# Layer 3's output stage in source order on three engines, with transposes one step behind normalizing and the first image read back during the convolution

## The chip, the cores and the metric

The kernel runs on one core of a Trainium2 chip. The metric is the device time of one execution in microseconds; the time of a kernel is the median of its runs. Names of engines as in the profile: PE is TensorE (PEld its weight loads), DVE is VectorE, ACT is ScalarE, POOL is GpSimd, SP is SyncE, which here only issues transfers.

## The reference

Eight images of 56 x 56 pixels with 192 channels go through four layers, each of the form x + layer(group norm(x)). Only the last matters here:

```python
def _L3_conv_ref(x, dw_kernel, dw_bias, ln_gamma, ln_beta, w0, b0, w1, b1, gamma):
    y = lax.conv_general_dilated(x, dw_kernel, (1, 1), 'SAME', feature_group_count=192, ...) + dw_bias
    mu = jnp.mean(y, axis=-1, keepdims=True)
    var = jnp.mean(jnp.square(y - mu), axis=-1, keepdims=True)
    y = (y - mu) * lax.rsqrt(var + EPS) * ln_gamma + ln_beta
    y = jnp.einsum('bhwc,cd->bhwd', y, w0) + b0
    y = jax.nn.gelu(y, approximate=False)
    y = jnp.einsum('bhwd,dc->bhwc', y, w1) + b1
    return y * gamma
...
x = x + _L3_conv_ref(_gn(x), ...)
```

The convolution is depthwise, 7 x 7. The layer norm goes over the 192 channels of each pixel. w0 widens 192 channels to 768, w1 narrows them again. All is float32.

## The kernel before, in words

One program does all four layers in stages, each with its own pools of tiles in SBUF and PSUM. A scheduler places the instructions of each engine: it takes them by priority as their inputs and their buffers come free by its own model of time, so the order on an engine is not that of the source. Each engine then works its queue in order. The pools hand out buffers by name: `bufs=2` means that the third tile of a name waits for the last use of the first.

Two stages of layer 3 are concerned.

**The convolution** (`convolve`, L988 to L1023). A loop over 12 groups of 16 channels. For each group SP loads the band matrix `wt` (4 MB, L997) and eight pieces `zc`, one for each image (L1002), from DRAM. PE does 64 matmuls (L1009), 16 for each four channels, for all images at once; DVE and ACT copy the sums to `yc` (L1019, L1021); SP writes `yc` to DRAM as `yd[b]`, one transfer of 224 KB for each image (L1023). `yd[b]` has 128 rows: the two halves of an image's row pairs with 64 places each. 28 columns (`NPAIR`) for each channel are pairs of image rows.

**The output stage** (L1297 to L1317). w0, w1 and the bias `dwb` are loaded on POOL's queue. `layer3_load` reads all 192 channels of one image back (`yl`, 2688 KB, two buffers), `layer3_image` reads its residual `x`. `layer3_norm` is a generator that yields between steps, so that the caller can strew it between others' work. For one image it

- adds the bias on POOL in four pieces (L1043),
- takes statistics of each of 28 columns on DVE (`bn_stats`, L189), one yield for each four,
- turns them into mean and variance with six small DVE instructions for all columns (`ln_var`, L196 to L203),
- takes the square root on ACT (L209), and reciprocal and shift on DVE (`ln_rows`, L210, L212),
- and for four blocks of four columns (two halves each; the last block has two): scales on DVE (`yt`, L1058, eight instructions), transposes on PE in three groups of four (`tp`, L1065, two PSUM buffers) and copies with scale and shift on ACT to `y` (L1076).

`layer3_out` takes an image in four tiles of 392 columns. In a tile, for six values of m, PE does 12 matmuls (`ph`, L1087) and ACT the Gelu (`hid`, L1091); after each second m the caller's `between` runs one step of the next image's `layer3_norm`. Then PE does three sums of 12 matmuls (`po`, L1098), ACT scales (`z`, L1103), DVE adds the residual (L1105), and SP writes the result (L1108). `ph` has two PSUM buffers, so the matmuls of m + 2 wait for the Gelu of m. In the trace each of these matmuls is two records, so a tile is 72 records of `ph` and 72 of `po`.

Square root and Gelu are in different function tables of ACT, so that a table load stands at each change between them. In the order that the scheduler made, the steps of images run ahead of the source: while image b is put out, the norm of image b + 1 is finished and that of image b + 2 begun, up to its square root, in ACT's queue ahead of the Gelus of image b.

Of the kernel before, what the change touches and what calls it, by code (L numbers as in the profile page):

```python
# [27 lines left out]
DPERM = [128 * c + 32 * (s % 4) + i for cs, ss in PASSES[:2] for s in ss for c in cs for i in range(32)]  # L28
DPERM += range(512, D1)
HEADS, HD, WN = 6, 32, 49  # L30
C2 = 384
EXP = 768

# [43 lines left out]
def kernel(ctx: ExitStack, tc: tile.TileContext, a: dict, out: bass.AP):  # L77
# [24 lines left out]
    def vec(name, i=0, rows=128):  # L102
        o = VOFF[name] + i
        return vecs[0:rows, o:o + 1]
# [78 lines left out]
    def run(steps):  # L183
        for _ in steps:
            pass

    def ln_pieces(st, yl, ns):
        for n in ns:
            nc.vector.bn_stats(st[:, n], yl[:, :, n])  # L189

    def ln_var(st, P, nch, pool):

        mean = pool.tile([P, NPAIR], F32, name="ln_mean")
        nc.vector.tensor_tensor(mean, st[:, :, 1], st[:, :, 4], ALU.add)  # L196
        d = pool.tile([P, NPAIR], F32, name="ln_d")
        nc.vector.tensor_tensor(d, st[:, :, 1], st[:, :, 4], ALU.subtract)
        nc.vector.tensor_tensor(d, d, d, ALU.mult)
        var = pool.tile([P, NPAIR], F32, name="ln_var")  # L200
        nc.vector.tensor_tensor(var, st[:, :, 2], st[:, :, 5], ALU.add)
        nc.vector.tensor_scalar(var, var, 1.0 / nch, None, ALU.mult)
        nc.vector.scalar_tensor_tensor(var, d, 0.25, var, ALU.mult, ALU.add)  # L203
        return mean, var

    def ln_rows(mean, var, P, eps, pool):

        rs = pool.tile([P, NPAIR], F32, name="ln_rs")
        nc.scalar.activation(rs, var, AF.Sqrt, bias=eps[0:P])  # L209
        nc.vector.reciprocal(rs, rs)  # L210
        mr = pool.tile([P, NPAIR], F32, name="ln_mr")
        nc.vector.scalar_tensor_tensor(mr, mean, -0.5, rs, ALU.mult, ALU.mult)  # L212
        return rs, mr


    def toeplitz_rows(psum, pool, rows):
# [676 lines left out]
    def layer2_norm(k, ml, rs, mr, pool, psum):  # L893


        n0 = 4 * k
        nn = min(4, PH - n0)
        nt = 2 * W * nn
        y = pool.tile([128, 3, 2, 8 * W], F32, name="y2")
        for s in range(2):  # L900
            yt = pool.tile([2 * W, 4, C2], F32, name="yt2")
            for i in range(nn):
                n = PH * s + n0 + i
                if i % 2 == 0:
                    nc.vector.tensor_scalar(yt[:, i], ml[:, :, n], rs[:, n:n + 1], mr[:, n:n + 1], ALU.mult, ALU.add)
                else:
                    nc.scalar.activation(yt[:, i], ml[:, :, n], AF.Identity, bias=mr[:, n:n + 1], scale=rs[:, n:n + 1])  # L907
            for m in range(3):
                tp = psum.tile([128, 4, 2 * W], F32, name="tp2")
                for i in range(nn):  # L910
                    nc.tensor.transpose(tp[:, i], yt[:, i, 128 * m:128 * m + 128], ident[0:2 * W, 0:2 * W])  # L911
                nc.scalar.activation(
                    y[:, m, s, 0:nt], tp[:, 0:nn].rearrange("p i n -> p (i n)"), AF.Identity,
                    bias=vec("be2", m), scale=vec("g2", m),
                )
        return y
# [68 lines left out]
                    to(zt[0:64, :, 1 + PH], tp[0:64, n2, 0], 1)  # L985
            nc.sync.dma_start(zd[b][:, 64 * j:64 * j + 64], zt)

    def convolve():  # L988

        band = a["band"]  # L990
        with ExitStack() as st:
            pool = st.enter_context(tc.tile_pool(reuse_waits="tile", name="cv", bufs=2))
            psum = st.enter_context(tc.tile_pool(reuse_waits="tile", name="cvp", bufs=3, space=PSUM))
            for g in range(C // CG):
# [26 lines left out]
                            nc.scalar.copy(dst, src)  # L1021
                for b in range(nimg):
                    nc.sync.dma_start(yd[b][:, cs], yc[:, b])  # L1023

    def layer3_load(b, pool):
        yl = pool.tile([OP, C, NPAIR], F32, name="yl")
        nc.sync.dma_start(yl, yd[b])
        return yl

    def layer3_image(b, pool):  # L1030
        x = pool.tile([128, 3, NH], F32, name="x3")
# [3 lines left out]
    def layer3_norm(yl, pool, psum, dwb):  # L1035


        y = pool.tile([128, 3, NH], F32, name="y3")
        yield y
        st = pool.tile([OP, NPAIR, 6], F32, name="ln_st")  # L1040
        for n in range(0, NPAIR, 7):
            ys = yl[:, :, n:n + 7]
            nc.gpsimd.tensor_tensor(ys, ys, dwb.unsqueeze(2).to_broadcast([OP, C, 7]), ALU.add)  # L1043
        for n in range(0, NPAIR, 4):
            yield
            ln_pieces(st, yl, range(n, n + 4))
        rows = ln_var(st, OP, C, pool)
        yield
        rs, mr = ln_rows(*rows, OP, eps6, pool)
        for i0 in range(0, PH, 4):  # L1050
            yield
            ni = min(4, PH - i0)

            yt = pool.tile([OP, 4, 3, 2, 64], F32, name="yt3")
            for i in range(ni):
                for s in range(2):
                    n = PH * s + i0 + i
                    nc.vector.tensor_scalar(  # L1058
                        yt[:, i, :, s], yl[:, :, n].rearrange("p (j c) -> p j c", j=3),
                        rs[:, n:n + 1], mr[:, n:n + 1], ALU.mult, ALU.add,  # L1060
                    )
            for j in range(3):
                tp = psum.tile([128, 4, OP], F32, name="tp3")
                for i in range(ni):
                    nc.tensor.transpose(  # L1065
                        tp[:, i], yt[:, i, j].rearrange("p s c -> p (s c)"), ident[0:OP, 0:OP]
                    )

                src = tp[:, 0:ni].rearrange("p i (s w) -> p i s w", s=2)
                dims = [list(z) for z in src.ap]  # L1070
                src = bass.AP(
                    src.tensor, src.offset + OP - 1,
                    [dims[0], dims[1], [-dims[2][0], 2], [-dims[3][0], W]],
                )
                dst = y[:, j, 2 * W * i0:2 * W * (i0 + ni)].rearrange("p (i s w) -> p i s w", s=2, w=W)
                nc.scalar.activation(dst, src, AF.Identity, bias=vec("be3", j), scale=vec("g3", j))  # L1076

    def layer3_out(b, y, x, pool, psum, between):

# [171 lines left out]
    with ExitStack() as st:  # L1251
# [5 lines left out]
        ml = [layer2_load(b, pool) for b in range(min(2, nimg))]  # L1257
        x = [load_halves(pool, x2[0], "x2o")]
        ln_pieces(ml[0][1], ml[0][0], range(NPAIR))
        rows = ln_rows(*ln_var(ml[0][1], 2 * W, C2, pool), 2 * W, eps5, pool)  # L1260
        y = layer2_norm(0, ml[0][0], *rows, pool, psum)
        steps = iter(())
        for b in range(nimg):
            slot = [0]

            def between():

                i, slot[0] = slot[0], slot[0] + 1
                if b + 1 < nimg and i < 8:
                    ln_pieces(ml[b + 1][1], ml[b + 1][0], range(NPAIR * i // 8, NPAIR * (i + 1) // 8))  # L1270
                if b + 1 < nimg and i == 7:
                    following.append(ln_var(ml[b + 1][1], 2 * W, C2, pool))
                for _ in range(1 if i < 5 else 2):
                    next(steps, None)

            following = []
            for k in range(4):

                if k < 3:
                    ahead = layer2_norm(k + 1, ml[b][0], *rows, pool, psum)  # L1280
                elif b + 1 < nimg:
                    rows = ln_rows(*following[0], 2 * W, eps5, pool)
                    ahead = layer2_norm(0, ml[b + 1][0], *rows, pool, psum)
                if k == 2 and b + 1 < nimg:
                    x.append(load_halves(pool, x2[b + 1], "x2o"))
                if k == 3 and b + 2 < nimg:
                    ml.append(layer2_load(b + 2, pool))
                layer2_out(k, y, x[b], psum, w_out, between)
                y = ahead
            run(steps)  # L1290
            nc.sync.dma_start(xd[b], x[b])
            steps = layer3_in(b, x[b], zp, pool, psum)
        run(steps)


    convolve()
    with tc.tile_pool(reuse_waits="tile", name="l3o", bufs=2) as pool, tc.tile_pool(reuse_waits="tile", name="l3op", bufs=2, space=PSUM) as psum:  # L1297
        w0 = resident("w0", nc.gpsimd, pool)
        w1 = resident("w1", nc.gpsimd, pool)
        dwb = pool.tile([OP, C], F32, name="dwb", bufs=1)  # L1300
        nc.gpsimd.dma_start(dwb, a["dw_b"].partition_broadcast(OP))
        yl = [layer3_load(b, pool) for b in range(min(2, nimg))]
        x = [layer3_image(0, pool)]
        steps = layer3_norm(yl[0], pool, psum, dwb)
        y = [next(steps)]
        for _ in steps:
            pass
        for b in range(nimg):
            if b + 2 < nimg:
                yl.append(layer3_load(b + 2, pool))  # L1310
            if b + 1 < nimg:
                steps = layer3_norm(yl[b + 1], pool, psum, dwb)
                y.append(next(steps))
                x.append(layer3_image(b + 1, pool))
            layer3_out(b, y[b], x[b], pool, psum, lambda: next(steps, None))
            for _ in steps:
                pass  # L1317

# [98 lines left out]
```

## Time and profile before

| | us |
|---|---|
| median of 3 runs | 6330.82 (6327.23 to 6345.44) |
| the profiled execution, its own time | 6351.08 |
| its span | 6349.2 |
| the convolution's matmuls (first to last) | 5072.0 to 5372.0 |
| first matmul `ph` of the output stage | 5418.1 |
| last matmul of the output stage | 6342.5 |
| PE busy over the span | 5569.1 (88%) |

Two stretches of the output stage, as busy time of PE in a stretch: from 5585 to 5609 us PE is busy 24.00 of 24 us at full clock, with nothing of the norm beside it; from 5664 to 5692 it is busy 19.31 of 28. In the convolution, from 5180 to 5330, PE is busy all but 0.3 us, at a DMA share of 0.90.

How to read it: a row of the timeline has start and length in us, engine, line, operation, output and inputs, their shapes, the number of instructions merged into it, and in brackets the idle time of that engine before it and what ended that time. A row of the waits has who waited, for whom, the sum in us, the number of times and the longest. A page's row of instructions has busy us and mean ns, then the idle time ahead of them with its releaser. Matmul ends are modelled, starts are measured.

### The profile page before, as it was taken

The numbers are of one execution on the slowest core, as the hardware profiler recorded it, in microseconds if no ns is written. First come the engines' busy times: TensorE is split into PE (matmuls) and PEld (weight loads), VectorE is DVE, ScalarE is ACT, GpSimd is POOL, SyncE is SP. The second block draws the span as 40 slices with busy tenths as digits, with TensorE's granted clock in tenths as the row PEclk, the third lists the DMA queues.
The fourth block names the chain that finished last, engine by engine and source line by source line (L and its number), as shares of the span: only waits on it lengthen the run. The fifth ranks groups of instructions, "written<-read, shape, count | busy, mean of one in ns | idle before, by whom it ended". The sixth has DMA issues, their size and how long they took to land. (4 is left out here: it accounts for less than half of the span.)

```text
span 6349.2 us, 126376 instructions
## 1 busy us (share of the span) xinstructions
PE 5569.1 (88%) x55636; PEld 3587.9 (57%) x55636; DVE 3439.3 (54%) x4752; ACT 2239.7 (35%) x2922; POOL 1302.1 (21%) x813
## 2 busy tenths in 40 slices
PE   6799989999999688888888598999588798789999
PEld 5677766666666345545445375777244498344444
DVE  5677765555665344444444486888688511532321
ACT  2334444443344233333332102555355300333333
POOL 1100034544444122122121102333110100110100
PEclk8899999999999888888888799999798799899999
DMA  6799886666665613444433675666667488121211
GB/s 166 185 221 210 188 262 263 260 253 240 240 252 194 88 33 55 60 58 63 55 48 44 103 266 208 224 228 233 153 203 208 170 305 305 64 67 56 70 54 27
DMA packets 1039131, 1013.10 MB, mean 160 GB/s; under 512 B 832104, under 2 KB 964372, under 8 KB 1011572
## 3 DMA queue, kind: packets, MB, share of 16 engines
q1 hardware_dynamic: 1028064, 954.17, 53.7%
q0 software_dynamic: 5648, 31.32, 1.5%
q10 hardware_dynamic: 4868, 19.52, 0.9%
q8 instruction: 437, 7.16, 0.5%
q14 instruction: 114, 0.93, 0.0%
HBM read 676.28 MB, written 345.08 MB: 161 GB/s over the span
## 5 line engine op out<-in xcount | busy, mean ns | idle before, releaser
L366 PE MATMUL qv<-w_qv_sb,xn 64*112 64x288 f32 x5376 | 722.2, 425 | 50.9 <-DVE act L372 47.6
L404 POOL COPY lc<-lt 128x896 f32<-128x896 f32 (+1 forms) x320 | 573.0, 1808 | 616.7 <-PE op L412 598.7
L366 PEld LDWEIGHTS qv<-w_qv_sb,xn 64*112 64x112 f32 x5376 | 535.5, 184 | 232.8 <-DVE act L372 64.7
L1087 PE MATMUL ph<-y,w_sb 64*128 64x392 f32 x2304 | 429.9, 511 | 49.1 <-ACT hid L1091 49.1
L373 ACT ACTIVATE act<-act 112x576 f32<-112x576 f32 x448 | 299.5, 682 | 461.7 <-DVE act L372 428.2
L1098 PE MATMUL po<-hid,w_sb 128*64 128x392 f32 x2304 | 395.1, 496 | 10.8 <-ACT hid L1091 10.8
L412 PEld LDWEIGHTS op<-rc,lc 128*56 128x56 f32 x9216 | 308.4, 136 | 127.6 <-issue 65.7
L412 PE MATMUL op<-rc,lc 128*56 128x56 f32 x9216 | 339.7, 222 | 46.0 <-POOL lc L404 24.2
L424 PE MATMUL pj<-xn,w_p_sb 64*128 64x392 f32 (+1 forms) x1920 | 373.0, 515 | 7.7 <-issue 4.7
L445 PE MATMUL y<-pp,w_o_sb 128*64 128x392 f32 (+1 forms) x1920 | 355.9, 503 | 20.4 <-DVE x L453 11.6
L372 DVE TENSOR_TENSOR act<-qv,b_qv 112x576 f32<-112x576 f32 x448 | 320.8, 751 | 86.1 <-PE qv L366 85.7
L1105 DVE TENSOR_TENSOR x<-x,z 128x392 f32<-128x392 f32 x96 | 55.8, 581 | 557.9 <-ACT z L1103 557.9
L1087 PEld LDWEIGHTS ph<-y,w_sb 64*128 64x128 f32 x2304 | 230.5, 194 | 224.1 <-ACT hid L1091 55.2
L404 ACT COPY rc<-rt 128x896 f32<-128x896 f32 (+1 forms) x160 | 256.9, 1606 | 230.7 <-PE op L412 216.0
L834 PE MATMUL cv<-zc,wt 128*128 128x224 f32 x1536 | 312.8, 355 | 27.9 <-DMA zc<-pd 27.9
L834 PEld LDWEIGHTS cv<-zc,wt 128*128 128x128 f32 x1536 | 290.5, 189 | 71.0 <-issue 54.9
L705 POOL TENSOR_TENSOR e<-e,mx 128x1176 f32<-128x1176 f32 x64 | 139.9, 2186 | 925.1 <-DVE mx L704 874.4
L655 PE MATMUL qk_ps<-xr,wg 64*96 64x392 f32 x1536 | 309.6, 511 | 14.9 <-ACT qk L661 13.3
L438 DVE TENSOR_TENSOR pp<-pp,ot 128x784 f32<-128x784 f32 (+1 forms) x160 | 154.6, 967 | 308.4 <-ACT pp L429 287.2
L1009 PE MATMUL cps<-zc,wt 128*128 128x224 f32 x1536 | 299.3, 356 | 23.1 <-DMA zc<-zd 22.5
L1009 PEld LDWEIGHTS cps<-zc,wt 128*128 128x128 f32 x1536 | 290.0, 189 | 32.5 <-issue 24.9
L847 POOL TENSOR_TENSOR rows<-rows,loc 128x896 f32<-128x896 f32 x96 | 228.1, 2377 | 390.2 <-ACT rows L843 262.8
(206 smaller groups left out, 9321.5 us busy)
## 6 DMA issues: line engine op xcount, KB each, us to landing
lt<-left SPq DMA_DIRECT2D x72, 1792.0 KB
rt<-right SPq DMA_DIRECT2D x72, 1792.0 KB
left<-qv SPq DMA_DIRECT2D x224, 252.0 KB
right<-qv SPq DMA_DIRECT2D x448, 126.0 KB
wt<-in_band_dram SPq DMA_DIRECT2D x24, 2048.0 KB
wt<-in_band_dram SPq DMA_DIRECT2D x12, 4096.0 KB
pd<-pt SPq DMA_DIRECT2D x8, 5568.0 KB
zc<-pd SPq DMA_DIRECT2D x192, 232.0 KB
```

Source lines behind the costliest of these rows:

```text
L366: nc.tensor.matmul(ps[s][:, which, 0:D1 // 2], xn[64 * s:64 * s + 64, j, bass.ts(i, 2 * W)], w_qv[64 * s:64 * s + 64, j, which, ns], start ...
L372: nc.vector.tensor_tensor(act, ps[s][:, :, 0:D1 // 2], b_qv[:, :, ns], ALU.add)
L373: nc.scalar.activation(act, act, AF.Silu)
L404: copy(c[:, 0:nu], raw.rearrange("p (w u d) -> p u d w", u=nu, d=64 // nu)[:, :, d0:d0 + 8])
L412: nc.tensor.matmul(op[64 * u:64 * u + W, i, :], lc[:, u, i], rc[:, u, i], start=True, stop=True)
L424: nc.tensor.matmul(ps[0:M, s, 0:TT], w_p[64 * s:64 * s + 64, j, d0:d0 + M], xn[64 * s:64 * s + 64, j, ts], start=(j == 0), stop=(j == 2),)
L445: nc.tensor.matmul(y[64 * s:64 * s + 64], w_o[0:M, c, 64 * j:64 * j + 64], pp[0:M, s], start=(c == gated[0][0]), stop=(c == gated[-1][0]),)
L655: nc.tensor.matmul(ps[s], wg[64 * s:64 * s + 64, j, c0:c0 + HC], xw[64 * s:64 * s + 64, j, gs], start=(j == 0), stop=(j == 2),)
L834: nc.tensor.matmul(dst, wt[:, c4 + i, 128 * q:128 * q + 128], zc[:, :, c4 + i, q:q + NPAIR], start=(q == 0), stop=(q == 1),)
L1009: nc.tensor.matmul(dst.rearrange("p (b n) -> p b n", n=NPAIR), wt[:, c4 + i, q * OP:(q + 1) * OP], zc[:, :, c4 + i, q:q + NPAIR], start=(q ...
L1087: nc.tensor.matmul(ps[:, s, 0:TT], w0[64 * s:64 * s + 64, j, m * 128:(m + 1) * 128], y[64 * s:64 * s + 64, j, ts], start=(j == 0), stop=(j ...
L1098: nc.tensor.matmul(ps[64 * s:64 * s + 64], w1[:, m, 64 * j:64 * j + 64], hid[:, m, s], start=(m == 0), stop=(m == 5),)
```

## The change

Four things are changed, all in layer 3.

1. `convolve` gets a tile `first` (image 0's `yl`) and `dwb`, both in a new pool on the other side of SBUF that lives from before the convolution. After each group's writes, POOL reads that group of image 0 back from DRAM and adds the bias to it. The whole load of image 0 on SP goes away. w0 and w1 stay on POOL's queue, and now stand behind the twelve read-backs and additions.
2. For image 0 (`dwb is None`) the norm works block by block: statistics, variance, root and scaling of four column pairs at a time. Its block 0 is done ahead of `layer3_out`, the others in `between` of tile 0.
3. In all images a block's transposes and copies come one step after its scaling; statistics go in five steps rather than seven. A norm of a later image has twelve steps, as many as `layer3_out` has calls of `between`.
4. `tc.manual_schedule` keeps PE, ACT and DVE in source order from there to the end; POOL and SP are still the scheduler's.

In the built order, for images 1 to 7, the root stands behind the Gelu of m = 1 in tile 2 of the image before, the transposes of block 0 behind m = 5 of tile 2, those of blocks 1, 2 and 3 behind m = 1, 3 and 5 of tile 3. On ACT a block's three copies stand directly behind the Gelus of those m. For image 0, the root of block k + 1 stands ahead of the copies of block k. The order of all stages before is the same as it was.

`ln_var` and `ln_rows` take their statistics with a halves axis (a view for layer 2), so that they can work on a part of the columns.

```diff
+IN_ORDER = {mybir.EngineType.PE, mybir.EngineType.Activation, mybir.EngineType.DVE}
...
-    def convolve():
+    def convolve(first, dwb):
...
                 for b in range(nimg):
                     nc.sync.dma_start(yd[b][:, cs], yc[:, b])
+                nc.gpsimd.dma_start(first[:, cs], yd[0][:, cs])
+                add_bias(first[:, cs], dwb[:, cs])
...
+    def add_bias(y, dwb):
+        nc.gpsimd.tensor_tensor(y, y, dwb.unsqueeze(2).to_broadcast(list(y.shape)), ALU.add)
...
     def layer3_norm(yl, pool, psum, dwb):
         y = pool.tile([128, 3, NH], F32, name="y3")
         yield y
         st = pool.tile([OP, NPAIR, 6], F32, name="ln_st")
-        for n in range(0, NPAIR, 7):
-            ys = yl[:, :, n:n + 7]
-            nc.gpsimd.tensor_tensor(ys, ys, dwb.unsqueeze(2).to_broadcast([OP, C, 7]), ALU.add)
-        for n in range(0, NPAIR, 4):
+        first = dwb is None
+        if not first:
+            for n in range(0, NPAIR, 7):
+                add_bias(yl[:, :, n:n + 7], dwb)
+            for k in range(5):
+                yield
+                ln_pieces(st, yl, range(NPAIR * k // 5, NPAIR * (k + 1) // 5))
+            rows = ln_var(in_halves(st), C, pool)
             yield
-            ln_pieces(st, yl, range(n, n + 4))
-        rows = ln_var(st, OP, C, pool)
-        yield
-        rs, mr = ln_rows(*rows, OP, eps6, pool)
-        for i0 in range(0, PH, 4):
+            rs, mr = ln_rows(*rows, eps6, pool)
+
+        def scaled(i0):
+            yt = pool.tile([OP, 4, 3, 2, 64], F32, name="yt3")
+            for i in range(min(4, PH - i0)):
+                for s in range(2):
+                    k = i if first else i0 + i
+                    nc.vector.tensor_scalar(
+                        yt[:, i, :, s], yl[:, :, PH * s + i0 + i].rearrange("p (j c) -> p j c", j=3),
+                        rs[:, s, k:k + 1], mr[:, s, k:k + 1], ALU.mult, ALU.add,
+                    )
+            return yt
+
+        ready = None
+        for i0 in range(0, PH + 4, 4):
             yield
...
+            if i0 < PH:
+                if first:
+                    ns = slice(i0, min(i0 + 4, PH))
+                    ln_pieces(st, yl, [PH * s + n for s in range(2) for n in range(ns.start, ns.stop)])
+                    rs, mr = ln_rows(*ln_var(in_halves(st)[:, :, ns], C, pool), eps6, pool)
+                following = scaled(i0)
+            if ready is not None:
+                i1 = i0 - 4
+                ni = min(4, PH - i1)
+                for j in range(3):
+                    tp = psum.tile([128, 4, OP], F32, name="tp3")
+                    for i in range(ni):
+                        nc.tensor.transpose(
+                            tp[:, i], ready[:, i, j].rearrange("p s c -> p (s c)"), ident[0:OP, 0:OP]
+                        )
...
+                    nc.scalar.activation(dst, src, AF.Identity, bias=vec("be3", j), scale=vec("g3", j))
+            ready = following
...
-    convolve()
-    with tc.tile_pool(reuse_waits="tile", name="l3o", bufs=2) as pool, tc.tile_pool(reuse_waits="tile", name="l3op", bufs=2, space=PSUM) as psum:
+    with ExitStack() as st:
+        lpool = st.enter_context(tc.tile_pool(reuse_waits="tile", name="l3y", bufs=2, side="right"))
+        dwb = lpool.tile([OP, C], F32, name="dwb", bufs=1)
+        nc.gpsimd.dma_start(dwb, a["dw_b"].partition_broadcast(OP))
+        yl = [lpool.tile([OP, C, NPAIR], F32, name="yl")]
+        convolve(yl[0], dwb)
+        pool = st.enter_context(tc.tile_pool(reuse_waits="tile", name="l3o", bufs=2))
+        psum = st.enter_context(tc.tile_pool(reuse_waits="tile", name="l3op", bufs=2, space=PSUM))
         w0 = resident("w0", nc.gpsimd, pool)
         w1 = resident("w1", nc.gpsimd, pool)
-        dwb = pool.tile([OP, C], F32, name="dwb", bufs=1)
-        nc.gpsimd.dma_start(dwb, a["dw_b"].partition_broadcast(OP))
-        yl = [layer3_load(b, pool) for b in range(min(2, nimg))]
         x = [layer3_image(0, pool)]
-        steps = layer3_norm(yl[0], pool, psum, dwb)
-        y = [next(steps)]
-        for _ in steps:
-            pass
+        if nimg > 1:
+            yl.append(layer3_load(1, lpool))
+        st.enter_context(tc.manual_schedule(engines=IN_ORDER))
+        own, steps = layer3_norm(yl[0], pool, psum, None), iter(())
+        y = [next(own)]
+
+        next(own), next(own), next(own)
+
+        def between():
+            next(own, None)
+            next(steps, None)
...
-            layer3_out(b, y[b], x[b], pool, psum, lambda: next(steps, None))
-            for _ in steps:
-                pass
+            layer3_out(b, y[b], x[b], pool, psum, between)
+            run(steps)
```

## The prediction, as put on record ahead of the result

> **What bounds the kernel now.** I read the page first, then the waits of each engine in layer 3's output stage (5372 to 6343 us), then the chain of waits there, then the timeline round the longest waits. The page says who is busy: the two matmul groups of this stage.
>
> ```profile
> span 6349.2 us, 126376 instructions
> ...
> L1087 PE MATMUL ph<-y,w_sb 64*128 64x392 f32 x2304 | 429.9, 511 | 49.1 <-ACT hid L1091 49.1
> ...
> L1098 PE MATMUL po<-hid,w_sb 128*64 128x392 f32 x2304 | 395.1, 496 | 10.8 <-ACT hid L1091 10.8
> ```
>
> The last column is TensorE's idle time: 59.9 us stand before ph and po, and Gelu (L1091) ends it. The waits of the stage show why Gelu is late, and a third idle time, for the first image's normalized rows:
>
> ```profile
> PE ph L1087 <- ACT hid L1091: 49.1, 6, 10.0
> PE tp L1065 <- DVE yt L1058: 40.8, 5, 39.4
> PE po L1098 <- ACT hid L1091: 10.8, 1, 10.8
> ACT ln_rs L209 <- DVE ln_var L203: 92.2, 8, 35.5
> ```
>
> ScalarE waits 92.2 us in the square root of layer norm. It is a queue in order, so Gelu stands behind. One such place, at the start of image 1:
>
> ```profile
> 5546.13 0.33 SPq L1027 DMA_DIRECT2D yl<-yd  x1
> 5555.79 10.70 POOL L1043 TENSOR_TENSOR yl<-yl,dwb 128x1344 f32<-128x1344 f32 x4 [109.51 <-DMA yl<-yd]
> 5572.33 0.32 ACT L209 ACTIVATE ln_rs<-ln_var,eps 128x28 f32<-128x28 f32 x1 [7.11 <-DVE ln_var L203]
> 5574.38 1.72 ACT L1091 ACTIVATE hid<-ph,vecs_sb 128x784 f32<-128x784 f32 x2
> 5575.35 4.91 PE L1087 MATMUL ph<-y,w_sb 64*128 64x392 f32 x18 [7.70 <-ACT hid L1091]
> ```
>
> The scheduler put the root of image b+2 (b = 1 here: image 3) ahead of the Gelus of image b. That image is loaded only once yl has a free buffer (5546), gets its bias on GpSimd, its statistics, and only then its root: TensorE stands 7.7 us, and more around it. The same row recurs at 5691, 5805, 5921 and 6037. Last, the start of the stage:
>
> ```profile
> 5372.63 0.53 ACT L1021 COPY yc<-cps 128x448 f32<-128x448 f32 x1 [5.62 <-DVE yc L1019]
> 5373.19 3.99 SPq L1023 DMA_DIRECT2D yd<-yc  x8
> 5377.29 1.16 SPq L1027 DMA_DIRECT2D yl<-yd  x2
> 5387.51 20.56 POOL L1043 TENSOR_TENSOR yl<-yl,dwb 128x1344 f32<-128x1344 f32 x8 [37.97 <-DMA yl<-yd]
> 5390.07 11.62 DVE L189 BATCH_NORM_STATS2 ln_st<-yl 128x6 f32<-128x192 f32 x28 [17.48 <-POOL yl L1043]
> 5418.09 1.67 PE L1087 MATMUL ph<-y,w_sb 64*128 64x392 f32 x2
> ```
>
> From the last convolution matmul (5372.0) to the first of ph, 46.1 us pass without one matmul of use.
>
> **What the skill says, and the trace.** "ScalarE: Activation LUTs", What ACT_TABLE_LOAD costs: 1283 ns and some 1380 ns of drain. The trace has the 1.28; Gelu starts 0.01 us after it (5573.09 and 5574.38), so I take no drain, and keep it as an upper bound. "SBUF — State Buffer", Who interferes with whom: a VectorE operation with two SBUF inputs blocks against a GpSimd operation that reads SBUF. The trace agrees: the six small ln_var steps take 0.9 us when GpSimd is idle (5467.57 to 5468.45) and 10.5 us while it adds bias (5435.80 to 5446.33), whereas statistics keep 0.415 us each. "TensorE: Matmul & The Clock Gate", What's actually happening: after an idle window TensorE runs at half rate for some 3.4 us. The trace agrees: eight transposes take 1.97 us at 5422.55 and 1.09 at 5541.26. "DMA: Bandwidth & Descriptors", Anatomy of one DMA: 2.0 us plus bytes/436e3 per us for a DMA from GpSimd. For the 112 KB of ema it gives 2.3, the trace 2.4.
>
> **The account of before.** A tile of 392 columns is 72 records of ph (12.05 us) and 72 of po (12.00): 24.05, an image of four 96.2. The stage, from 5372.0 to the last matmul (6342.5), is: start 46.1; image 0 from 5418.1 to 5562.9, 144.8; images 1 to 5 to 6140.6, 115.55 each; image 6, with the transposes of image 7 but no root in the way, 105.0; image 7 96.9. Sum 970.5.
>
> **Start of the stage.** The first image comes back in twelve pieces of 224 KB during the convolution; only the last lies on the path. Its write starts at 5373.2; I take 2.6 us (2.0 plus 0.5 by the formula; the trace bounds it at 4.1, for the load that waits for it was issued at 5377.3). Then the DMA on GpSimd: 0.5 for issue, 2.6, and 0.6 to 1 because seven more yd writes share the engines: landed 5379.7. Bias for 448 elements: 2.57 x 448/1344 = 0.9. So 5380.7. Then VectorE and ScalarE in source order: 8 statistics 3.35, ln_var 0.9, root 0.35, two rows 0.6, 8 yt at 0.547 4.4 (TensorE transposes behind), then the second block's 8 statistics 3.35: 5393.7. The second block's root stands ahead of the first block's copies in ScalarE's queue, so ln_var of block 2 is on the path, and image 1's bias (4 x 2.6 on GpSimd) is running then: yl[1] was asked for at 5377.3 and, sharing the engines with w0 and w1 (now issued at 5380.7, behind the last bias), lands about 5391. ln_var ends when GpSimd does, 5402 (5394.6 if GpSimd is idle then; at most 5404.3, four of its operations behind 5393.7). Root 0.3 and three copies with a transpose between them 2.1: first ph 5404.5, a start of 32.5 us. w0 took 6.0 us to land before; even at half rate it is there at 5393.
>
> **First image.** Three more blocks are normalized inside tile 0. Each time ScalarE takes two table loads (1.28) and waits for a VectorE chain: rows 0.6, yt 4.4, statistics 3.35, ln_var 0.9, root. Following the three queues: ph m0 and m1 at cold clock to 5410.3; copies of block 1 wait for the root at 5413.0; m2 and m3 end 5418.6; block 2's at 5421.2; m4 and m5 end 5426.7; block 3, then po 5428.7 to 5440.7. Tile 0 costs 36.2, 12.15 above clean. Tiles 1 to 3 and image 1's norm: 72.15 plus 1.05 (root) plus 10.5 (transposes), both below: 83.7. Image 0: 119.9 for 144.8.
>
> **An image in the steady state.** VectorE and ScalarE no longer run an image ahead, so a root never waits for a load: yl[b+2] is asked for when yt of yl[b] is done, and used an image later. The root now stands after ph m1 of tile 2: load 1.28, root 0.32, load 1.28 in front of the Gelu of m2, while TensorE has two m of work (3.95). Gelu m2 ends 5.0 after m1; stall 1.05 (3.8 with drains). ln_var is done in tile 1, so the root doesn't wait. Transposes: of three groups of four, the third waits for the first copy, which stands behind the Gelu of the same m: 0.11 + 0.92 + 0.67 + 0.1 = 1.8, then 0.6, restart 0.3: 2.7 a block. Before, with a ph pair in the gap, a block cost (31.77 - 24.05)/3 = 2.57 (6213.28 to 6245.05); that pair took 0.85 instead of 0.33 there, which is why its loss is small. Last half block: Gelu first, 2.4. So 3 x 2.7 + 2.4 = 10.5 (8 to 14). Is yt in time? Root ends 2.7 after m1, eight yt at 7.7, TensorE asks at 9. Yes, by 1.3. Image: 96.2 + 10.5 + 1.05 = 107.8. Images 1 to 5 save 7.8 each, 38.8; image 6 has the new order's cost without an old stall, +2.8; image 7 96.2, -0.7.
>
> **Other edits.** GpSimd: twelve DMAs and adds ahead of w0, w1: hidden in the convolution but for the last. SP loses one yl load: yl[1] is now first behind the yd writes, the two images x behind it. Its load of yl[2] waits for the first image's last yt (5418), with image 0's outputs queued behind, which come only after 5432. In the convolution the readback adds 2.75 MB; taken at nothing, since TensorE is busy 50.0 of 50 us there with the DMA engines at 0.88 to 0.90. If that cover is gone, 0.7 us a group, 8 us. The order of all stages before is unchanged. Smaller ln tiles: nothing.
>
> **Sum.** -13.6 (start) - 24.9 (image 0) - 38.8 + 2.8 - 0.7 = -75.2. Against the profiled execution: 6351.1 - 75.2 = 6275.9. It was 20.3 above the median of the runs, so the median goes 6330.8 - 75.2 = 6255.6.
>
> **Rivals.** (a) Hand-offs cost more: each block 3.9, the root 3.8 with drains: 10.5 becomes 14.1 and the image 114.1, 6.3 x 7 = 44 given back: 6300. For it: source order leaves no filler; against: ph in the gap bought only 0.2. (b) The start gains nothing: the readback is late (shared engines) or bias and ln_var interlock longer, start 46: 6269. (c) Slower: the convolution becomes DMA-bound. The point is 24.8 us a group; the engines are idle 10%, 2.5 us. The readback needs 0.7 at 325 GB/s. Were it 11.1 us of all engines, by taking turns in small packets with zc loads that are sent only at 5311.87 to 5317.2 for use at 5322.4, eleven groups would lose 8.6 each: 6255.6 + 95 = 6351, slower. Against it: w0 and w1 (1.7 MB on the same queue) ran in the convolution at 5347.9, and TensorE was busy 41.94 of 42 us. (d) The scheduler reorders anyway: excluded for three engines by the built order, where each root stands in tile 2.
>
> **How the numbers follow.** Forecast 0.75 (own range 6238 to 6276: start 6 us either way, image 2.5 x 7, convolution up to 8); (a) 0.13, of which 0.04 so bad that it is within 0.3%; (b) 0.08; (c) 0.04. 0.3% is about what a measurement of this kernel can tell from no change. Faster 0.75 + 0.09 + 0.08 = 0.92, same 0.04, slower 0.04. The range takes in (b) and a part of (a): 6236 to 6284.
>
> **What would show it.** ScalarE's wait in ln_rs falls from 92 to under 45 us, all of it in the first image's four roots, and the seven later roots don't wait; TensorE's idle before ph for hid has no 7 to 10 us row after image 0; first ph about 32 us after the last convolution matmul; images 107.8 us apart; convolution unchanged within 8 us. Wrong, if images come 112 or more apart, or if groups of the convolution stretch.

## The result, and the profile after

| | before | after |
|---|---|---|
| median of 4 runs each, us | 6329.52 (6327.23 to 6345.44) | 6251.93 (6247.04 to 6264.17) |
| ratio | | 0.9877, 95% interval 0.986 to 0.9894 |
| the profiled execution: its own time, span | 6351.08, 6349.2 | 6264.17, 6262.4 |
| first to last matmul of the convolution | 5071.99 to 5371.94 (300.0) | 5064.91 to 5367.62 (302.7) |
| first `ph`, last matmul of the output stage | 5418.09, 6342.48 | 5397.82, 6255.26 |

The change makes the kernel 77.6 us faster by the medians (forecast: 75). The span of the profiled execution lost 86.8: 7.1 ahead of the convolution, in stages whose instructions the change leaves the same; the convolution gave 2.8 back; the output stage, counted as in the prediction from the last convolution matmul to the last matmul, went from 970.5 to 887.6, or -82.9; 0.4 came back behind the last matmul.

The page after, the same two groups of matmuls. The last column is again TensorE's idle time just before them:

```profile
span 6262.4 us, 126450 instructions
...
L1115 PE MATMUL ph<-y,w_sb 64*128 64x392 f32 x2304 | 399.2, 499 | 6.4 <-ACT hid L1119 6.4
...
L1126 PE MATMUL po<-hid,w_sb 128*64 128x392 f32 x2304 | 386.3, 494 | 0.0
```

The 59.9 us that stood before `ph` and `po` are 6.4. The waits of the stage (in all, times, longest):

```profile
ACT ln_rs L212 <- DVE ln_var L204: 26.7, 2, 14.9
PE ph L1115 <- ACT hid L1119: 6.4, 7, 0.9
PE tp L1092 <- DVE yt L1071: 17.0, 4, 15.3
PE tp L1092 <- ACT y L1103: 33.7, 32, 9.5
```

ScalarE waited 92.2 us for the square root's input; what is left is two waits, both at the start of the stage. No wait of TensorE for a Gelu is over 0.92 us. New is a wait of the third group of transposes for the first copy: in the steady state, between 5600 and 6190, it comes 23 times for 15.5 us together.

The start of the stage, where 46.1 us passed without useful matmuls:

```profile
5368.88 3.99 SPq L1030 DMA_DIRECT2D yd<-yc  x8
5371.12 0.55 POOL L1031 DMA_DIRECT2D yl<-yd  x1 [19.63 <-DMA yd<-yc]
5375.30 0.93 POOL L1040 TENSOR_TENSOR yl<-yl,dwb 128x448 f32<-128x448 f32 x1 [3.63 <-DMA yl<-yd]
5385.22 10.33 POOL L1040 TENSOR_TENSOR yl<-yl,dwb 128x1344 f32<-128x1344 f32 x4 [7.97 <-DMA yl<-yd]
5389.28 1.13 DVE L199 TENSOR_TENSOR ln_mean<-ln_st 128x8 f32<-128x8 f32 x1
5390.53 2.54 DVE L201 TENSOR_TENSOR ln_d<-ln_d 128x8 f32<-128x8 f32 x1
5393.18 2.40 DVE L203 TENSOR_SCALAR ln_var<-ln_var 128x8 f32<-128x8 f32 x1
5395.81 0.30 ACT L212 ACTIVATE ln_rs<-ln_var,eps 128x8 f32<-128x8 f32 x1 [14.89 <-DVE ln_var L204]
5397.82 5.96 PE L1115 MATMUL ph<-y,w_sb 64*128 64x392 f32 x24
```

The read of the last piece of image 0 is issued 2.24 us after its write, and the piece has its bias at 5376.2, 8.6 us after the last convolution matmul. Before, the four additions of image 0 ended at 5397.8, 25.9 us after it (the row of eight additions in the prediction takes in image 1). The first `ph` comes 30.2 us after the last convolution matmul. Of these, 6.5 go into `ln_var` of the second block (5389.28 to 5395.78; the first block's took 0.95), while GpSimd adds the bias of image 1.

A steady image, at the place where the root now stands (tile 2), and one block of transposes:

```profile
5465.55 0.92 ACT L1119 ACTIVATE hid<-ph,vecs_sb 128x784 f32<-128x784 f32 x1 [1.06 <-PE ph L1115]
5466.48 1.28 ACT L212 ACT_TABLE_LOAD   x1
5467.78 0.32 ACT L212 ACTIVATE ln_rs<-ln_var,eps 128x28 f32<-128x28 f32 x1
5468.11 1.28 ACT L1119 ACT_TABLE_LOAD   x1
5469.41 1.72 ACT L1119 ACTIVATE hid<-ph,vecs_sb 128x784 f32<-128x784 f32 x2
5470.38 4.22 PE L1115 MATMUL ph<-y,w_sb 64*128 64x392 f32 x24 [0.92 <-ACT hid L1119]
...
5492.96 1.09 PE L1092 MATMUL tp<-ident,yt 128*128 128x128 f32 x8
5494.66 0.66 PE L1092 MATMUL tp<-ident,yt 128*128 128x128 f32 x4 [0.61 <-ACT y L1103]
5495.25 4.22 PE L1115 MATMUL ph<-y,w_sb 64*128 64x392 f32 x24
```

The root waits for nothing; for its two table loads TensorE waits 0.92 us. A block costs TensorE 5495.25 - 5492.96 = 2.29. Tiles 0 and 1 of such an image last 24.05 each, tile 2 27.53, tile 3 30.91: 106.5 for 115.55.

### The profile page after: what moved, and what is told of

Its sections match the earlier page's. It is cut to its first block, busy times and chain, and to the rows that moved or that the text cites. A ratio compares the mean times of both kernels' runs of the same rounds, so it can differ in the third digit from the quotient of the medians.

```text
span 6262.4 us, 126450 instructions
## 1 busy us (share of the span) xinstructions
PE 5524.5 (88%) x55636; PEld 3577.2 (57%) x55636; DVE 3441.0 (55%) x4776; ACT 2243.7 (36%) x2929; POOL 1312.8 (21%) x833
## 5 line engine op out<-in xcount | busy, mean ns | idle before, releaser
L1115 PE MATMUL ph<-y,w_sb 64*128 64x392 f32 x2304 | 399.2, 499 | 6.4 <-ACT hid L1119 6.4
L1133 DVE TENSOR_TENSOR x<-x,z 128x392 f32<-128x392 f32 x96 | 72.3, 753 | 520.8 <-ACT z L1131 520.8
L1115 PEld LDWEIGHTS ph<-y,w_sb 64*128 64x128 f32 x2304 | 220.8, 189 | 176.7 <-issue 26.8
```

Source lines behind the costliest of these rows:

```text
L1115: nc.tensor.matmul(ps[:, s, 0:TT], w0[64 * s:64 * s + 64, j, m * 128:(m + 1) * 128], y[64 * s:64 * s + 64, j, ts], start=(j == 0), stop=(j ...
```

## The experiments

In the stages ahead of the convolution all kernels do the same (three of them load two weights there in addition), yet the convolution begins anywhere from 5052 to 5089 us. So each is read in its trace from the convolution's first matmul on, where two kernels that were profiled twice repeat to within 1 us (the changed kernel 1190.4 and 1191.2, the one with three edits 1160.2 both times), and its time is given as a ratio to the kernel before, timed again beside it. "Start" is the time from the last convolution matmul to the first `ph`. In microseconds:

| kernel | convolution | start | image 0 | images 1 to 6, each | image 7 | first matmul of the convolution to the last | ratio, 95% |
|---|---|---|---|---|---|---|---|
| before | 300.0 | 46.1 | 144.8 | 115.5; 105.1 the last | 96.8 | 1270.5 | 1 |
| after | 302.7 | 30.2 | 121.9 | 106.5 | 96.3 | 1190.4 | 0.9877 (0.986 to 0.9894) |
| order left to the scheduler | 302.9 | 22.2 | 143.9 | 116.2; 105.7 the last | 96.3 | 1251.7 | 0.9969 (0.9952 to 0.9985) |
| order alone | 300.1 | 54.7 | 110.8 | 110.8 to 112.0 | 98.2 | 1232.8 | 0.9942 (0.9921 to 0.9964) |
| image 0 read late | 300.1 | 40.5 | 121.4 | 106.5 | 96.3 | 1197.5 | 0.9886 (0.9871 to 0.9901) |
| transposes in the same step | 302.9 | 23.3 | 145.5 | 110.9 to 112.5 | 96.3 | 1240.0 | 0.995 (0.9933 to 0.9966) |
| before without the root | 300.5 | 45.6 | 132.8 | 105.1 | 96.8 | 1206.2 | 0.9918 (0.99 to 0.9936) |
| root in tile 1 | 303.3 | 30.9 | 120.3 | 105.3 | 96.3 | 1182.9 | 0.9863 (0.9841 to 0.9885) |
| no bias for image 1 | 303.3 | 24.6 | 121.2 | 106.5 | 96.3 | 1184.7 | 0.9861 (0.9842 to 0.988) |
| copies ahead of Gelu | 302.9 | 30.9 | 120.4 | 105.4 | 96.3 | 1183.0 | 0.9866 (0.9846 to 0.9886) |
| first image spread | 302.6 | 20.7 | 116.8 | 106.5 | 96.3 | 1175.7 | 0.987 (0.9848 to 0.9893) |
| these three edits together | 302.7 | 20.7 | 115.1 | 104.2 | 96.3 | 1160.2 | 0.9847 (0.9819 to 0.9874) |

### Was it the root? The kernel before without it

```diff
-        nc.scalar.activation(rs, var, AF.Sqrt, bias=eps[0:P])
+        if eps is eps6:
+            nc.vector.tensor_scalar(rs, var, 1e-6, None, ALU.add)
+        else:
+            nc.scalar.activation(rs, var, AF.Sqrt, bias=eps[0:P])
```

> The kernel before with layer 3's square root replaced by one addition on VectorE, so that ScalarE has no instruction that waits for image b+2 (this leaves the square root out: rows are scaled by 1/(var + eps)). Main theory (before, TensorE lost its time because the root stood ahead of Gelu in ScalarE's queue until that image was loaded, biased and reduced): no row of 7 to 10 us ahead of ph is left, images 1 to 5 come about 107 to 109 us apart: minus 45 to 57, about 6280. Rival (the load, bias and statistics themselves hold the transposes, whatever ScalarE does): within 10 us of 6330.

Measured: images 1 to 5 at 105.1, minus 10.4 each; image 0 minus 12; in all -64.3 in the trace, more than the 45 to 57 expected (by the medians it is 49.7, which lies within), and the order is still the scheduler's. TensorE's one wait for a Gelu in the stage is in image 0:

```profile
PE ph L1090 <- ACT hid L1094: 10.2, 1, 10.2
PE tp L1068 <- DVE yt L1061: 40.3, 5, 38.9
```

So the theory of the prediction holds for what was lost: loads, bias and statistics come as late as before (`ln_var` of image 3 ends 10.3 us after the first `ph` of image 1, before 9.4), but nobody stands behind them. The second row is the start, unchanged.

The loss was more than the wait, as image 2 of the kernel before shows. The second row and the third, in a fence of its own, sum up a stretch: its ends and length, the busy us of PE, PEld, DVE, ACT and POOL with their instructions in brackets, the share of TensorE's full clock that the profile records as granted, DMA share and GB/s. The third is the changed kernel, from image 1 to the last matmul.

```profile
5691.07 10.01 PE L1087 MATMUL ph<-y,w_sb 64*128 64x392 f32 x48 [8.69 <-ACT hid L1091]
5684.60:5694.80 10.20, 3.73 (x12) 2.16 (x14) 8.50 (x24) 3.75 (x5) 0.00 (x0) 0.50 0.37 87
```
```profile
5519.70:6255.20 735.50, 713.92 (x4286) 360.31 (x4284) 229.15 (x468) 270.53 (x342) 42.74 (x16) 1.00 0.19 58
```

TensorE waits 8.69 us, and the 48 records of `ph` behind the wait take 10.01 us at a clock of 0.50 in part; in the changed kernel 48 of them take 8.17 (at 5461.28). So of the 10.8 us that this tile lost against the kernel without the root, some 1.8 are a lower clock.

One more thing follows: at 105.1 the scheduler's order, freed of the root, is better than the new source order (106.5). Its transposes with `ph` between them cost 105.1 - 96.2 = 8.9 an image, those in source order 105.3 - 96.2 = 9.1 (from the run with the root out of the way, below): the same.

### Was it the order? All but the order, and the order alone

The first is the changed kernel without one line, the second the kernel before with that line around the output stage.

```diff
-        st.enter_context(tc.manual_schedule(engines=IN_ORDER))
```

> The changed kernel without the line that keeps three engines in source order (the read-back in the convolution, the first image in blocks and the deferred transposes stay). Main theory (the source order is what takes the square root of image b+2 out of the way of Gelu of image b): the scheduler puts the roots ahead again, ScalarE waits 60 us or more in ln_rs, images 1 to 5 are about 114 us apart instead of 106.5, some 40 us come back: about 6292. Rival (the read-back and the first image in blocks are the gain): about 6252, images 106.5 apart. Rival (the deferred transposes are the gain, whatever the order): under 6262.

Measured: 61.3 of the 80.1 us come back, 21 more than expected: images at 116.2 instead of 114, and image 0 with its start 14 longer. The waits and one place at the start of image 1:

```profile
ACT ln_rs L212 <- DVE ln_var L204: 111.0, 11, 14.1
PE ph L1115 <- ACT hid L1119: 40.5, 6, 7.8
```
```profile
5508.61 10.40 POOL L1040 TENSOR_TENSOR yl<-yl,dwb 128x1344 f32<-128x1344 f32 x4 [82.18 <-DMA yl<-yd]
5529.02 0.32 ACT L212 ACTIVATE ln_rs<-ln_var,eps 128x28 f32<-128x28 f32 x1 [13.59 <-DVE ln_var L204]
5532.75 11.14 PE L1115 MATMUL ph<-y,w_sb 64*128 64x392 f32 x48 [7.29 <-ACT hid L1119]
```

It is the row of the kernel before again: a root with 13.59 us of waiting, and TensorE behind it. The rivals that gave the gain to the read-back, the blocks or the deferred transposes are out: with all three, but without the order, 18.8 of the 80.1 us are left. No run takes the blocks alone out.

> The kernel before with the output stage in source order on TensorE, VectorE and ScalarE, nothing else changed. Main theory: the roots no longer stand ahead of Gelu, images come about 109.5 us apart (96.2, a root, and 12 to 13 for transposes that wait for yt made in the same step) instead of 115.55; the start is 10 us longer, since the whole first image is normalized ahead of the first ph: 7 x 6 - 10 plus what image 0 saves (10 to 20): about 6280. Rival (order alone gains nothing, the transposes have to be deferred for it): 6330 or slower.

Measured: -37.7, not -50. The start is 8.5 longer, as expected, and image 0 is 34 shorter, more than expected; but the images come only down to 111.5. TensorE has a new wait:

```profile
PE tp L1066 <- DVE yt L1059: 69.2, 29, 38.8
```

38.8 of it are the start; the rest, about 4 us an image, are transposes that ask for `yt` in the same step, the first of them 2.4 us too early, and the granted clock falls with it (0.50 from 6191.8 to 6198.5). The expectation priced this wait at about 2 us an image. Order takes the root away and puts another wait in its place.

### What the deferral is worth

```diff
-        for i0 in range(0, PH + 4, 4):
+        for i0 in range(0, PH, 4):
...
-                following = scaled(i0)
+                ready = scaled(i0)
```

> The changed kernel with each block's transposes in the step that normalizes it, not one behind. Main theory: TensorE then waits in each block for yt, which VectorE begins only when the step before ends on its queue: some 4 to 5 us an image for images 1 to 7, 13 in tile 0, less 8 at the start, where the second block is no longer ahead of the first ph: about 6288. Rival (VectorE runs far enough ahead that the deferral is worth nothing): about 6252 or less.

Measured: +49.6 against the changed kernel, 13 more than expected: 5.5 an image instead of 4.5, and tile 0 57.6 instead of 39.4. Tile 2 is 33.2 to 34.8 for 27.53. There TensorE goes at VectorE's pace, one transpose for two `yt`, and the granted clock is 0.50 from 5712.7 to 5719.4:

```profile
PE tp L1092 <- DVE yt L1071: 58.9, 49, 15.8
```
```profile
5709.81 0.33 PE L1092 MATMUL tp<-ident,yt 128*128 128x128 f32 x1 [0.54 <-DVE yt L1071]
5710.88 0.33 PE L1092 MATMUL tp<-ident,yt 128*128 128x128 f32 x1 [0.74 <-DVE yt L1071]
```

Deferral without the order gains little (the run without the order, -18.8 with the read-back and the blocks in it), and order without deferral less than half (-37.7; with read-back and blocks -30.5). Together they give -80.1. They are one edit.

### What the read-back is worth

```diff
-                nc.gpsimd.dma_start(first[:, cs], yd[0][:, cs])
-                add_bias(first[:, cs], dwb[:, cs])
...
+        nc.sync.dma_start(yl[0], yd[0])
+        for n in range(0, NPAIR, 7):
+            add_bias(yl[0][:, :, n:n + 7], dwb)
```

> The changed kernel with the first image read back whole after the convolution by SP's queue and biased in four pieces on GpSimd, as before; the blocks of the first image and the order stay. Main theory (the read-back takes load and bias of the first image off the path): the first ph comes 46 to 50 us after the last convolution matmul instead of 30: plus 15 to 18, about 6269; the convolution gets 0 to 3 us shorter. Rival (the start is bounded by w0 and by GpSimd's bias of image 1): under plus 5, 6252 to 6257.

Measured: the start is 40.5, 10.3 longer and not 15 to 18, and the convolution 2.6 shorter: +7.2 in all. The image is loaded in 10.2 us and its first block needs three of the four additions:

```profile
5364.06 0.57 SPq L1332 DMA_DIRECT2D yl<-yd  x1
5374.26 10.29 POOL L1038 TENSOR_TENSOR yl<-yl,dwb 128x1344 f32<-128x1344 f32 x4 [38.51 <-DMA yl<-yd]
5385.39 0.30 ACT L212 ACTIVATE ln_rs<-ln_var,eps 128x8 f32<-128x8 f32 x1 [25.39 <-DVE ln_var L204]
```

The expectation took the load and all four additions as in the kernel before; working in blocks already takes a part of that off the path. What the read-back costs is a wait of the convolution. In the changed kernel three groups behind the first start late for their `zc`, where before none did:

```profile
5117.76 49.55 PE L1016 MATMUL cps<-zc,wt 128*128 128x224 f32 x256 [0.73 <-DMA zc<-zd]
5167.78 49.59 PE L1016 MATMUL cps<-zc,wt 128*128 128x224 f32 x256 [0.48 <-DMA zc<-zd]
5318.10 49.52 PE L1016 MATMUL cps<-zc,wt 128*128 128x224 f32 x256 [0.78 <-DMA zc<-zd]
```

These three make 2.0 of the 2.8 us. All ten profiles with the read-back have a convolution of 302.6 to 303.5, the four without it 300.0 to 300.5. (The edit takes the pieces' bias out of the convolution as well; that TensorE waits for a transfer speaks for the read-back.)

### What is left: four edits of the changed kernel

The ratios of these four (0.9861 to 0.987) have intervals that overlap with that of the changed kernel, so what each is worth is read from its trace alone.

**The root at the end of tile 1**, ahead of `po` instead of between two Gelus:

```diff
-            rows = ln_var(in_halves(st), C, pool)
+            rs, mr = ln_rows(*ln_var(in_halves(st), C, pool), eps6, pool)
             yield
-            rs, mr = ln_rows(*rows, eps6, pool)
```

> The changed kernel with the root of an image at the end of tile 1's last step, where TensorE still has po of the tile ahead, instead of inside tile 2. Main theory (the two ACT_TABLE_LOADs round the root cost TensorE 0.9 us an image): 7 x 0.9 less, about 6246; no idle row ahead of ph in tile 2. Rival (the wait moves to the Gelus at the end of tile 1): within 2 us of 6252.

Measured: tile 2 26.34 for 27.53, images 105.3: 1.2 an image, -8.0 in the stage. TensorE has no wait for Gelu left; the second table load lies under the start of the next `ph`:

```profile
5551.94 1.28 ACT L212 ACT_TABLE_LOAD   x1
5562.89 12.12 PE L1114 MATMUL ph<-y,w_sb 64*128 64x392 f32 x72
5563.70 1.28 ACT L1118 ACT_TABLE_LOAD   x1
```

**No bias for image 1**, to see what it costs `ln_var` of the second block:

```diff
-            for n in range(0, NPAIR, 7):
+            for n in range(0, NPAIR if biased else 0, 7):
```

> The changed kernel without the bias addition of image 1 on GpSimd (leaves that addition out for image 1 alone), so that GpSimd is idle while VectorE does ln_var of the first image's second block. Main theory (those six small operations take 6.5 us instead of 1.0 because GpSimd is adding in SBUF): the first ph comes 5.5 us earlier and z adds in tile 0 take 0.57 instead of 1.6 to 2.7: about 6246. Rival (w0, landed 8 us ahead of the first ph, or the copies hold the start): 6250 to 6252.

Measured: the start 24.6, minus 5.6, as expected. The additions of `z` in tile 0 are not down to 0.57: they take 1.78, 0.86 and 2.40, for GpSimd is then adding the bias of image 2 (5428.32 to 5439.32). The operation that took 2.54 us takes 0.17:

```profile
5395.15 0.17 DVE L201 TENSOR_TENSOR ln_d<-ln_d 128x8 f32<-128x8 f32 x1
```

**The step ahead of the odd Gelu**:

```diff
+                ahead = m % 2 and (t == 3 or (t == 2 and m == 5))
+                if ahead:
+                    between()
...
-                if m % 2:
+                if m % 2 and not ahead:
```

> The changed kernel with the step (scale, transposes, copies) ahead of the odd Gelu of the pair instead of behind it, for the blocks in tile 2 and tile 3. Main theory (a block costs 2.26 us because its copies stand behind a Gelu that waits for TensorE, the third group of transposes waiting for the first copy): 0.5 a block and 0.9 in the half block less, 2 us an image, about 6238. Rival (the Gelu that is now behind the copies delays the next ph by the same time): within 3 us of 6252.

Measured: 1.1 an image, half of what was expected, -7.6 in the stage. A block is 2.06 us for 2.29 (5509.03 to 5511.09), because that Gelu had begun 0.1 us after the first transpose and stood in the copy's way only by 0.2:

```profile
5509.03 1.09 PE L1092 MATMUL tp<-ident,yt 128*128 128x128 f32 x8
5509.73 2.20 ACT L1103 ACTIVATE y<-tp,vecs_sb 128x448 f32<-128x448 f32 x3 [1.64 <-PE tp L1092]
5510.51 0.66 PE L1092 MATMUL tp<-ident,yt 128*128 128x128 f32 x4 [0.38 <-ACT y L1103]
5511.09 4.22 PE L1115 MATMUL ph<-y,w_sb 64*128 64x392 f32 x24
```

**The first image spread over three tiles**: w0 and w1 are loaded ahead of the convolution, block 0 is transposed at once, blocks 1 to 3 come in tiles 0 to 2, each scaled after one pair of Gelus and transposed two pairs later.

```diff
+        w0 = resident("w0", nc.gpsimd, lpool)
+        w1 = resident("w1", nc.gpsimd, lpool)
...
+        if first:
+            for i0 in range(0, PH, 4):
...
+                ready = scaled(i0)
+                if i0:
+                    yield
+                    yield
+                turned(ready, i0)
+                yield
+            return
```

> The changed kernel with w0 and w1 loaded before the convolution, the first image's block 0 transposed as soon as it is scaled, and blocks 1 to 3 spread over tiles 0 to 2 (scaled after one pair of Gelus, transposed after the next but one). Main theory (the start waits for the second block's statistics and ln_var under GpSimd's bias and not for a transfer): first ph about 20 us after the last convolution matmul instead of 30, tile 0 6 us shorter: about 6236. Rival (the three blocks cost later what they save at the start): within 4 us of 6252.

Measured: the start 20.7, tile 0 28.98 for 39.41, of which tiles 1 and 2 give 5.4 back: -14.6 in the stage. Tile 0 gains more than expected, for its pairs of `ph` run faster; the second of them has a granted clock of 1.00 (5418.1 to 5422.3). First this kernel, then the second and third pair of the changed one, each pair 24 records:

```profile
5412.23 5.52 PE L1127 MATMUL ph<-y,w_sb 64*128 64x392 f32 x24
...
5418.12 4.22 PE L1127 MATMUL ph<-y,w_sb 64*128 64x392 f32 x24 [0.37 <-ACT hid L1131]
```
```profile
5407.77 5.91 PE L1115 MATMUL ph<-y,w_sb 64*128 64x392 f32 x24
...
5417.50 5.92 PE L1115 MATMUL ph<-y,w_sb 64*128 64x392 f32 x24
```

The stage is not the whole account. With w0 and w1 loaded ahead of the convolution, its first matmul comes later behind the stage before: it waits 26.7 us for `zc`, where it waits 22.4 to 22.5 in all eleven profiles without the early loads. First this kernel, then the changed one:

```profile
5088.90 31.41 PE L1016 MATMUL cps<-zc,wt 128*128 128x224 f32 x149 [26.65 <-DMA zc<-zd]
```
```profile
5064.91 52.11 PE L1016 MATMUL cps<-zc,wt 128*128 128x224 f32 x256 [22.43 <-DMA zc<-zd]
```

These 4.2 us lie ahead of what the table counts, so the edit is worth some 10 us and not 14.6.

### The three edits together

> The three edits together: root at the end of tile 1, the step ahead of the odd Gelu, and the start of the run with w0 and w1 early. Main theory (the three losses lie in different places and add): 10 + 6 + 6 + 14, about 6216. Rival (they share a resource, ScalarE's queue): 6230 or more.

Measured: -30.2 in the trace, where the three alone gave 8.0 + 7.6 + 14.6 = 30.2: they add. The total expected was 36, mainly since the step ahead of the odd Gelu was sized at twice its worth. Here too the first convolution matmul waits longer (26.8 us), which leaves some 26 of the 30. The ratio's interval overlaps that of the changed kernel, from another chip; so the two were timed side by side on one chip.

> The changed kernel itself, on the same chip and between the same runs as the kernel with the three edits together, since their ratios to the kernel before (0.9877 and 0.9847) came from different chips and their intervals overlap. If the loss of the stage seen in the profile is all there is: 0.9875 of before, and the stage 887.6 us again.

> The kernel with the three edits together, beside the changed kernel. If the 30.2 us by which its output stage is shorter in the profile reach the end: 30 us below the changed kernel, 0.983 of before. Rival (the time of the stages ahead, which the edits do not touch, hides or eats it): within 10 us of the changed kernel.

Measured: the changed kernel 6282.4 us, 0.9881 (0.986 to 0.9901); the three edits 6254.41 us, 0.9826 (0.9801 to 0.9852), with the kernel before at 6354.48. The two differ by 28.0 us, the stage by 887.7 - 857.65 = 30.1; the wait ahead of the convolution takes 4.2 of that back (26.67 for 22.43). The version with the three edits is faster than both kernels.

## Why the prediction was right, and where its sizes were off

The forecast named the cause, and the runs bear it out: the root of image b + 2 in ScalarE's queue ahead of the Gelu of image b (out by itself: -64.3), and the order as what removes it (put back: +61.3). Term by term:

| step of the prediction | predicted | measured |
|---|---|---|
| start | -13.6 | -16.0 |
| image 0 | -24.9 | -22.9 |
| images 1 to 5 | -38.8 | -45.0 |
| image 6 | +2.8 | +1.5 |
| image 7 | -0.7 | -0.6 |
| convolution | 0 | +2.8 |
| sum (of unrounded terms) | -75.2 | -80.1 |

That the medians (-77.6) came within 3 us of the forecast is in part luck: the misses of the terms, from -6.2 to +2.8, partly cancel, and the stages ahead, which were not changed, vary by more than that from one execution to another (the convolution begins between 5052 and 5089).

**Start.** The chain is the predicted one. From the write to the biased piece it took 7.35 us for 7.5 predicted (2.24 to the issue of the read, 4.10 to its landing, 0.93 for the bias). `ln_var` of the second block did get caught by GpSimd; its end, 26.9 us after the write, was put at 28.8, because image 1 landed 1.5 us earlier than taken, counted from the write. The run without that bias shows the price of it, 5.6. The weights w0 and w1 took 13.5 and 20.0 us to land, where 6 to 12 were allowed; w0 was still there 8 us before its use.

**Image 0.** Tile 0 was put at 36.2 and took 39.4. The wait for the copies came out as worked out: they begin 2.71 and 2.55 us after the transposes of blocks 1 and 2 (5403.71 to 5406.42, 5413.61 to 5416.16), where 2.7 and 2.6 were predicted. The step that failed is the next one, from the start of the copies to the end of the following pair of `ph`: 5.6 and 5.5 us in the prediction, 7.19 both times in the trace (to 5413.61 and 5423.35). `ph` goes on 1.35 us after the copies began, and the pair itself takes 5.84. The prediction does not split its 5.6, but its own figures give it with the pair at full speed: 0.67 + 0.1 + 0.6 + 0.3 for the first copy, the third group and the restart, and 3.95 for the pair. Only the very first pair was put at cold clock. In fact the later pairs had a lower clock as well, 0.71 on average:

```profile
5407.80:5413.60 5.80, 5.80 (x25) 3.02 (x24) 5.73 (x15) 2.92 (x3) 0.00 (x0) 0.71 0.01 3
```

Tiles 1 to 3 took 82.5 for 83.7.

**Images.** 106.5 for 107.8. The root costs 1.2, where 1.05 was predicted. A block costs 2.29, not 2.7: 1.70 to the third group and 0.59 for it fit, the added "restart 0.3" and a tenth do not exist. So each block was some 0.4 dearer in the forecast, and with it the five images some 6 us.

**Convolution.** "Taken at nothing", with 8 us as the price if the cover is gone. It is 2.8. Three groups of twelve wait for `zc`, 0.5 to 0.8 each, 2.0 together; the rest is in shorter stops for which the profile names no transfer. Each wait is near the 0.7 a group that the prediction gave for the transfer; that this is more than chance is not shown. The prediction's witness for full cover, the loads of w0 and w1 at 5347.9, was a weak one: from 5330 to 5372 the DMA share was 0.62, not 0.90.

**Rivals.** Dearer hand-offs, no gain at the start and a convolution bound by its transfers did not come, though the last one is there in small. That the scheduler would reorder is true: without the line it does. What the prediction did not separate is order and deferral. It priced the new order with deferral in it, which was right for this change; that order by itself would have kept under half of the gain is known only from the runs.

## What to carry to other kernels

When one engine's queue holds an instruction for work far ahead, ask what it waits for and who stands behind it on that engine: here 0.3 us of square root cost 10 us an image, though everything it waited for was hidden. An order by hand takes such a wait away and the scheduler's slack with it, so plan in the same edit who then asks too early (here TensorE for `yt`), and put a step between producer and consumer. Divide the stage into start, first and steady item and count each, for the gains then add and the misses can be found.

## What the runs showed that was not expected

- **Small VectorE operations beside GpSimd.** Not each of the six waits: 1.13, 2.54 and 2.40 us for `ln_mean`, `d * d` and the scaling of `ln_var`, 0.16 or 0.17 for the others. Each long one ends about when one of GpSimd's additions (10.33 / 4 = 2.58 us) ends. The Trainium skill, "SBUF — State Buffer", Who interferes with whom, names operations with two SBUF inputs and, in its two-port mode, `tensor_scalar`; both kinds are among the three. But not every `tensor_scalar` is caught: in the run with the order left to the scheduler, ten scalings `yt` of 192 elements began while GpSimd was adding and took 0.62 us each, as the others did.
- **TensorE's clock after short gaps.** In tile 0 of the changed kernel, gaps of some 4 us with 1.75 us of transposes in them were each followed by 24 records of `ph` in 5.9 us instead of 4.22, though no single idle time was over 2.4 us; the granted clock was 0.50 from 5408.3 to 5411.6, within the second pair. After the steady state's gaps of 2.3 us they take 4.22, at a granted clock of 1.00. Nor did TensorE always recover within the 3.4 us that the prediction quotes: in the kernel before, from the first `ph` at 5418.1 to 5435.4, the profile has it busy for all 17.30 us, and the clock stayed at 0.50.
- **Loads from GpSimd's queue under load.** 1152 KB took 13.5 us and 576 KB behind it 20.0, with one image and two residuals on SP's queue at the same time.
- **Steadiness by stage.** The output stage of the changed kernel took 887.6 and 887.7 us in two profiles from different chips, while its convolution began at 5064.9 and 5078.4. Why the unchanged stages vary was not examined.
